# Layer 2 keeps h in the order (batch, node) in a four-layer graph network

## The chip, the cores and the metric

The kernel runs on one core of one Trainium2 chip. The metric is the device time of one execution in microseconds, the median of several runs; smaller is better. Beside the timed runs one execution was recorded by the hardware profiler. All data is fp32.

## The reference

The input x has 128 batches of 64 nodes with 256 features; adj is a 64 by 64 matrix. Four layers follow each other, each as `x = layernorm(x + layer(x))`. Layer 0 is a graph convolution with two linear maps and batch norms. Layer 1 is a spectral step, an attention over the nodes and an MLP. Layer 2, which the change touches, is cut here to what matters:

```python
h = relu(einsum('ts,bsh->bth', adj, x @ Wg0 + bg0))
h = relu(einsum('ts,bsh->bth', adj, h @ Wg1 + bg1))
for p in range(1, MAX_SKIP + 1):                    # 1, 2, 3, 4
    nw = Tv // p                                    # windows of p nodes
    wins = h[:, :nw * p, :].reshape(Bv * nw, p, Hd)
    last = _lstm_last(Wih[p - 1], Whh[p - 1], bih[p - 1], bhh[p - 1], wins)
    idx = jnp.arange(nw) * p + (p - 1)
    h = h.at[:, idx, :].set(last.reshape(Bv, nw, Hd))
```

For each p the 64 nodes of a batch are cut into windows of p nodes. An LSTM runs over the p nodes of every window, and its last state replaces h at the window's last node. Layer 3 is a graph attention that reads `layernorm(x + h)`.

## The kernel before

The 128 batches are cut into 16 blocks of 8 batches (512 rows), and for layer 2 into 4 groups of 32 batches. The state h of a group lies in one SBUF tile `Hg[g]` with the features on the partitions (two halves c of 128) and 64 x 32 positions on the free axis. The view `hT` gives these positions the order (c, node, batch): for one node the 32 batches are neighbours, and the next node is 32 elements (128 bytes) further on.

A planner written in Python (`flow`) sets the order of all instructions. Each piece of work is a generator that yields steps with an engine, an assumed cost, and the number of PSUM tiles and temporary buffers that it takes. The planner picks the next step by these costs and by the free buffers; the engines then run their instructions in the order in which they were written. Several streams compete: graph convolution blocks, LSTM units, weight loads, and the last blocks (layer 3). The final three LSTM units have a stream of their own that is marked urgent.

The parts that matter here:

- `gcn_block(i)` makes h of one block and runs the LSTM for p = 1 on it (one step, no window). Its `out_of` writes the result to `hT_block(i)`, line L1357, on DVE.
- `unit(p, g, w0, nw, b0, nb)` runs the LSTM for p = 2, 3 or 4 on nw windows and nb batches of a group. `units_of` gives 8 units for p = 2 (16 windows each), 8 for p = 3 (12 or 9 windows), and 5 for p = 4 (three of 16 windows and 32 batches, two of 16 windows and 16 batches). `x_of(s, q)` is the view of h at node s of every window, for part q of the unit; units of 32 batches have two parts. `out_of` writes the last state at node p - 1 of every window, line L1389, on DVE.
- `lstm` does the work of a unit. In its first step (s = 0) it multiplies h by the input weights: L1055, with `x_of(0, q)` as the moving operand, as in `T.matmul(out, stationary, moving)`. In the steps after that, a unit with two parts u and v uses products of sums and differences: L1127, of which the product named `A11` has `x_u`, a view of h, as its moving operand; the others move temporaries, save that L1147 (POOL, `T1 = x_v - x_u`) and L1173 (DVE, `T3 = h_v - x_v`) read h to make them.
- `plain_steps` does these steps for the two units of one part (p = 4, group 3): L1264 moves `x`, a view of h, and L1266 moves the LSTM's own state.
- `last_block(i, t0, nt)` is layer 3 for a block, or for half of one in group 3. It first brings h into the order (batch, node) with two copies on ACT (L1467) into a temporary buffer, then transposes it on PE by `to_tm` (L359; the chunk of h is the stationary operand, the identity is moved) and adds it to x (L1478). Later lines: L314 layer normalization on ACT, L308 a power on POOL, L1507 products, L1544 exponentials, L1574 the sum of attention and x.

In the profile's names h is the tile of a group, wL, x and wB hold the weights of p = 1 and 3, 2, and 4 at those products, and t, x, h, rows, wA, wL and others are lent out as temporary buffers too.

Of the kernel before, what the change touches and what calls it, by code (L numbers as in the profile page):

```python
# [11 lines left out]
ALU = mybir.AluOpType  # L12
# [3 lines left out]
P = 128  # L16
B, N, D = 128, 64, 256
# [16 lines left out]
def kernel(ctx: ExitStack, tc: tile.TileContext, a: dict, out: bass.AP):  # L34
    nc = tc.nc
    V, S, G, T = nc.vector, nc.scalar, nc.gpsimd, nc.tensor

    def bc_mid(ap, n):

        return ap.unsqueeze(1).to_broadcast([ap.shape[0], n, ap.shape[1]])  # L40
# [5 lines left out]
    def tm(s):  # L46

        return s.rearrange("p (t d) -> p t d", t=NT)

    def fm(s):  # L50

        return s.rearrange("p (c k) -> p c k", c=2)
# [59 lines left out]
    def mark(*key):  # L112
        done[key] = Clock.end
# [7 lines left out]
    def step(e, us, ps=0, sl=0, waits=True, at=None, tbl=None):  # L121

        return (e, us, ps, sl, waits, at, tbl)
# [83 lines left out]
    def ctile(shape, name, pool=cp):  # L212
        return pool.tile(shape, F32, tag=name, name=name)
# [6 lines left out]
    Hg = [ctile([P, 4 * NT * D], f"h{g}", big) for g in range(NG)]  # L220
    Hs = [Hg[i // 4][:, (i % 4) * NT * D : (i % 4 + 1) * NT * D] for i in range(NBLK)]
    H = [fm(s) for s in Hs]
    hT = [t.rearrange("p (c n b) -> p c n b", c=2, n=N) for t in Hg]
    XD = [dram.tile([P, NT, D], F32, tag=f"xd{i}", name=f"xd{i}") for i in range(NBLK)]

    PS = Stock([ctile([P, NT * D], f"ps{j}", psp) for j in range(4)])
    mem = Stock([ctile([P, NT * D], f"t{j}", big) for j in range(TEMPS)])
# [96 lines left out]
    def joined(ps, n=2 * NT):  # L324

        return ps.rearrange("p (s g e) -> p g s e", s=2, e=N)[:, :n]

    def runs(ap):

        if len(ap.shape) == 2:  # L330
            return ap.rearrange("p (g s e) -> p g s e", s=2, e=N)
        return ap.rearrange("p t (c s e) -> p (t c) s e", s=2, e=N)

    def aggregate(ps, y, mT):


        for c in range(2):
            for t in range(NT):
                for f, to in enumerate(halves):
                    for s, h in enumerate(halves):  # L340
                        T.matmul(  # L341
                            part(ps, s, c * NT + t)[to],
                            y[h, t, c * P + f * N : c * P + (f + 1) * N],
                            mT[h, h],
                            start=True,
                            stop=True,
                        )
# [7 lines left out]
    def to_tm(ps, yT):  # L355

        for t in range(ps.shape[1]):
            for c in range(2):
                T.transpose(ps[:, t, c * P : (c + 1) * P], yT[:, c, t * P : (t + 1) * P], ident)  # L359

    def mm_fm(ps, w, yT, nk, off=0):

        for c in range(2):
            for k in range(nk):
                T.matmul(  # L365
                    ps[:, c, :],
                    w[:, k, (off + c) * P : (off + c + 1) * P],
                    yT[:, k, :],
                    start=(k == 0),
                    stop=(k == nk - 1),  # L370
                )

    def mm_tm(ps, yT, w, nk):

        for t in range(NT):
            for k in range(nk):
                T.matmul(  # L377
                    ps[:, t, :],
                    yT[:, k, t * P : (t + 1) * P],
                    w[:, k, :],  # L380
                    start=(k == 0),
                    stop=(k == nk - 1),
                )

    def by_chunk(ap):
        return ap.rearrange("(k p) m -> p k m", p=P)
# [19 lines left out]
    with c0:  # L406
# [299 lines left out]
        for k, w in zip(("Wc", "Wq", "Wk", "Wv", "Wo", "W1", "W2"), (Wc, Wq, Wk, Wv, Wo, W1, W2)):  # L706
            src = by_chunk(a[f"L1_gnn_{k}"])
# [312 lines left out]

    def hT_block(i):

        return hT[i // 4][:, :, :, (i % 4) * 8 : (i % 4) * 8 + 8]

    def lstm(p, n, parts, x_of, out_of):

# [279 lines left out]
    def gcn_block(i):  # L1306
        yield step("T", 1.15, ps=1, sl=1)
        ps = PS.take()
        s_a = mem.take()
        aggregate(PS[ps], X[i], bdAT)  # L1310
        yield step("Q", 4.0, waits=False)
        nc.sync.dma_start(XD[i], X[i])
        mem.add([Xs[i]], Clock.end, part=("x", i // 2) if i < 8 else None)
        mark("x", i)
        yield step("S", 1.05, ps=-1)
        S.copy(runs(mem[s_a]), joined(PS[ps]))
        PS.give(ps)
        yield step("T", 3.45, ps=1, sl=1)
        ps = PS.take()
        s_h1 = mem.take()  # L1320
        mm_tm(tm(PS[ps]), fm(mem[s_a]), Wg0, 2)
        mem.give(s_a)
        yield step("V", 1.25, ps=-1)
        h1 = tm(mem[s_h1])
        V.tensor_tensor(h1, tm(PS[ps]), bc_mid(rb0, NT), ALU.add)
        PS.give(ps)
        yield step("S", 1.05)
        S.activation(mem[s_h1], mem[s_h1], AF.Relu)
        yield step("T", 1.15, ps=1, sl=1)
        ps = PS.take()  # L1330
        s_a = mem.take()
        aggregate(PS[ps], h1, bdAT)
        mem.give(s_h1)
        yield step("S", 1.05, ps=-1)
        S.copy(runs(mem[s_a]), joined(PS[ps]))
        PS.give(ps)
        yield step("T", 3.45, ps=1, sl=1)
        ps = PS.take()
        s_h2 = mem.take()
        mm_fm(fm(PS[ps]), Wg1, fm(mem[s_a]), 2)  # L1340
        mem.give(s_a)
        yield step("V", 1.4, ps=-1)
        h2 = fm(mem[s_h2])
        for c in range(2):
            V.tensor_tensor(
                h2[:, c, :].rearrange("p (b n) -> p b n", b=8),
                fm(PS[ps])[:, c, :].rearrange("p (b n) -> p b n", b=8),
                bc_mid(rb1[:, c, :], 8),
                ALU.add,
            )  # L1350
        PS.give(ps)
        t = yield step("S", 1.05)
        S.activation(mem[s_h2], mem[s_h2], AF.Relu)  # L1353


        def out_of(q, c, o, th):
            V.tensor_tensor(  # L1357
                hT_block(i)[:, c, :, :].rearrange("p n b -> p b n"), o, th, ALU.mult
            )

        yield step("T", 0.0)
        h2 = h2.rearrange("p c (b n) -> p c b n", b=8)
        yield from lstm(1, TB, [(slice(0, TB), 8)], lambda s, q: h2, out_of)
        yield step("V", 0.0)
        mem.give(s_h2)
        mark("p", 1, i)

    def unit(p, g, w0, nw, b0, nb):
        src = hT[g][:, :, w0 * p : (w0 + nw) * p, b0 : b0 + nb].rearrange("p c (w q) b -> p c w q b", q=p)

        hn = nw * nb // 2
        even = nw % 2 == 0
        parts = [(slice(q * hn, (q + 1) * hn), nw // 2 if even else nw) for q in range(2)]
        if nb < BG:
            parts = [(slice(0, 2 * hn), nw)]

        def half(ap, q):

            if len(parts) == 1:
                return ap  # L1380
            if even:
                return ap[..., q * nw // 2 : (q + 1) * nw // 2, :]
            return ap[..., q * nb // 2 : (q + 1) * nb // 2]

        def x_of(s, q):
            return half(src[:, :, :, s, :], q)

        def out_of(q, c, o, th):
            V.tensor_tensor(half(src[:, c, :, p - 1, :], q), o, th, ALU.mult)  # L1389

        yield from lstm(p, nw * nb, parts, x_of, out_of)
        mark("p", p, g, w0, nw, b0, nb)
# [63 lines left out]
    def last_block(i, t0=0, nt=NT):  # L1456
# [3 lines left out]
        x = tm(mem[s_x])[:, :nt, :]  # L1460
        nc.sync.dma_start(x, XD[i][:, t0 : t0 + nt, :])
        r = nt / NT
        yield step("S", 2.2 * r, sl=1)
        s_h = mem.take()
        hb = fm(mem[s_h])[:, :, : nt * P]
        for c in range(2):
            S.copy(  # L1467
                hb[:, c, :].rearrange("p (b n) -> p b n", n=N),
                hT_block(i)[:, c, :, 2 * t0 : 2 * (t0 + nt)].rearrange("p n b -> p b n"),
            )  # L1470
        yield step("T", 0.9 * r, ps=1)
        ps = PS.take()
        px = tm(PS[ps])[:, :nt, :]
        to_tm(px, hb)
        mem.give(s_h)
        mark("read", i)
        yield step("V", 0.1 + 1.2 * r, ps=-1)
        V.tensor_tensor(x, px, x, ALU.add)  # L1478
# [6 lines left out]
        px = fm(PS[ps])[:, :, : nt * P]  # L1485
# [99 lines left out]
    seq, n = [], 0  # L1585
# [73 lines left out]
    for p, g in [(2, g) for g in range(NG)] + [(3, 0), (3, 1), (4, 0), (3, 2), (4, 1), (3, 3), (4, 2), (4, 3)]:  # L1659
        if p == 2:  # L1660
            need = [("p", 1, i) for i in range(4 * g, 4 * g + 4)] + [("begun", NBLK - 1)]
        else:
            need = units_of(p - 1, g)
        for u in units_of(p, g):
            units.append((lambda p=p, need=need: ready(("w", p), *need), lambda u=u: unit(*u[1:]), 7))
# [5 lines left out]
    def last_of(i, *part):  # L1671
        return (lambda: ready(("wx",), *units_at_end(i)), lambda: last_block(i, *part), 3)
# [66 lines left out]
```

## Time and profile before

| what | value |
|---|---|
| median of 3 runs (lowest to highest) | 2407.23 us (2405.26 to 2409.41) |
| profiled execution, its time | 2409.44 us |
| its span | 2407.7 us |
| mean granted TensorE clock | 0.982 |
| instructions | 40,603 |
| L1467, the copies ahead of layer 3 | 24 of 512 elements, 16 of 256; first at 1859.6, last at 2375.8 us |
| L1357, p = 1 writing h | 32 of 512 elements, from 464.3 to 1356.7 us |
| first product of a p = 2 unit | 1214.9 us |
| first product of a p = 4 unit | 1718.1 us |

PE is TensorE's multiplication and PEld its loading of stationary operands; DVE is VectorE, ACT ScalarE, POOL GpSimd, and SP the engine that starts most transfers. A group of instructions is shown as line, engine, operation, out<-in, shape and count, then busy time and the mean duration of one in ns, then how long the engine was idle just before and who ended that. Every `T.matmul` of the program appears as two MATMUL records. The records of matmuls that follow each other overlap, so the time of one is read from the distance between starts.

### The profile page before, as it was taken

The numbers are of one execution on the slowest core, as the hardware profiler recorded it, in microseconds if no ns is written. First come the engines' busy times: TensorE is split into PE (matmuls) and PEld (weight loads), VectorE is DVE, ScalarE is ACT, GpSimd is POOL, SyncE is SP. The second block draws the span as 40 slices with busy tenths as digits, with TensorE's granted clock in tenths as the row PEclk, the third lists the DMA queues.
The fourth block names the chain that finished last, engine by engine and source line by source line (L and its number), as shares of the span: only waits on it lengthen the run. The fifth ranks groups of instructions, "written<-read, shape, count | busy, mean of one in ns | idle before, by whom it ended". The sixth has DMA issues, their size and how long they took to land.

```text
span 2407.7 us, 40603 instructions
## 1 busy us (share of the span) xinstructions
PE 2287.2 (95%) x16916; PEld 1759.9 (73%) x16916; DVE 1287.7 (53%) x2904; ACT 1187.4 (49%) x2189; POOL 591.7 (25%) x441
## 2 busy tenths in 40 slices
PE   8999788999989999999999999999999999998997
PEld 4548665666665666666667788899999888887785
DVE  4557678566483474744643433454444444455546
ACT  2257643544434544335453443444444653468766
POOL 0012134232242232331321222222221222122122
PEclk9999899999999999999999999999999999999998
DMA  6100301000000000001000000000001000001111
GB/s 162 49 1 1 111 23 49 28 10 10 1 12 17 10 10 10 1 10 36 36 19 27 18 1 1 17 2 1 1 1 36 1 10 9 19 27 66 40 36 45
DMA packets 42633, 57.91 MB, mean 24 GB/s; under 512 B 6224, under 2 KB 35536, under 8 KB 42448
## 3 DMA queue, kind: packets, MB, share of 16 engines
q1 hardware_dynamic: 41344, 54.22, 7.0%
q8 instruction: 133, 2.18, 0.4%
q10 hardware_dynamic: 1104, 1.08, 0.1%
q14 instruction: 52, 0.43, 0.1%
HBM read 38.52 MB, written 16.78 MB: 23 GB/s over the span
## 4 chain that ended last, share of the span: by engine, by line
PE 60%; DVE 16%; ACT 7%; POOL 3%; issue 2%; POOLq 0%; ACTq 0%; DVEq 0%
PE ps L1127 26%; PE ps L1055 11%; PE ps L365 7%; PE ps L377 4%; PE ps L938 4%; DVE ln_st L272 3%; ACT x L314 2%; PE ps L808 2%; POOL ln_rs L308 1%; PE ps L1507 1%; DVE x L300 1%; PE ps L341 1%; DVE ln_mv L273 1%; PE ps L353 1%; DVE ln_nm L311 1%
## 5 line engine op out<-in xcount | busy, mean ns | idle before, releaser
L1127 PE MATMUL ps<-x,x 128*128 128x256 f32 x928 | 225.0, 380 | 0.7 <-DVE t L1195 0.7
L1127 PEld LDWEIGHTS ps<-x,x 128*128 128x128 f32 x928 | 173.5, 190 | 24.9 <-issue 1.6
L314 ACT ACTIVATE x<-x,ln_nm,ln_rs 128x256 f32<-128x256 f32 x212 | 112.3, 592 | 133.3 <-DVE ln_nm L311 131.9
L1127 PE MATMUL ps<-t,x 128*128 128x256 f32 x672 | 163.7, 380 | 0.0
L1127 PEld LDWEIGHTS ps<-t,x 128*128 128x128 f32 x672 | 126.4, 190 | 17.1 <-DVE x L1195 0.8
L308 POOL TENSOR_TENSOR ln_rs<-ln_rs,neghalf 128x4 f32<-128x4 f32 (+1 forms) x72 | 71.2, 990 | 212.0 <-DVE ln_rs L274 186.4
L365 PE MATMUL ps<-t,W1T 128*128 128x512 f32 x256 | 117.8, 607 | 0.0
L1055 PE MATMUL ps<-h,wL 128*128 128x192 f32 (+2 forms) x480 | 103.9, 371 | 4.8 <-ACT h L1353 4.8
L272 DVE BATCH_NORM_STATS2 ln_st<-x 128x6 f32<-128x256 f32 x260 | 99.7, 403 | 0.4
L1055 PEld LDWEIGHTS ps<-h,wL 128*128 128x128 f32 x480 | 75.6, 192 | 29.9 <-issue 22.5
L294 POOL TENSOR_TENSOR ln_rs<-ln_rs,neghalf 128x4 f32<-128x4 f32 x32 | 36.9, 1153 | 217.1 <-DVE ln_rs L274 217.0
L1055 PE MATMUL ps<-h,x 128*128 128x256 f32 x384 | 86.7, 380 | 2.2 <-ACT t L1067 1.8
L1067 ACT ACTIVATE t<-ps,bih 128x512 f32<-128x512 f32 (+3 forms) x98 | 57.2, 634 | 55.8 <-PE ps L1055 55.1
L1203 ACT ACTIVATE x<-x,bih 128x512 f32<-128x512 f32 (+2 forms) x69 | 44.6, 648 | 80.3 <-DVE x L1193 80.0
L1186 DVE COPY x<-ps 128x256 f32<-128x256 f32 (+2 forms) x69 | 26.1, 378 | 108.4 <-PE ps L1127 107.6
L365 PEld LDWEIGHTS ps<-t,W1T 128*128 128x128 f32 x256 | 47.6, 195 | 49.6 <-issue 49.5
L365 PE MATMUL ps<-t,wA 128*128 128x512 f32 x160 | 76.8, 626 | 5.5 <-ACT t L784 5.5
L1055 PEld LDWEIGHTS ps<-h,x 128*128 128x128 f32 x384 | 72.6, 190 | 12.9 <-ACT t L1067 2.2
L1186 DVE COPY t<-ps 128x256 f32<-128x256 f32 (+2 forms) x51 | 18.8, 373 | 103.8 <-PE ps L1127 103.5
L1067 ACT ACTIVATE x<-ps,bih 128x512 f32<-128x512 f32 (+3 forms) x86 | 51.5, 650 | 40.6 <-PE ps L1055 40.4
L273 DVE BATCH_NORM_AGGREGATE ln_mv<-ln_st 128x2 f32<-128x6 f32 x448 | 71.3, 167 | 0.0
L1193 DVE TENSOR_TENSOR x<-ps,x 128x512 f32<-128x512 f32 (+2 forms) x69 | 41.4, 602 | 53.0 <-PE ps L1127 43.6
(714 smaller groups left out, 5713.2 us busy)
## 6 DMA issues: line engine op xcount, KB each, us to landing
t<-in_x_dram SPq DMA_DIRECT2D x26, 512.0 KB, 4.3
xd<-x SPq DMA_DIRECT2D x16, 512.0 KB, 2.6
x<-xd SPq DMA_DIRECT2D x8, 512.0 KB, 3.3
out_dram<-x SPq DMA_DIRECT2D x8, 512.0 KB, 2.9
h<-in_x_dram SPq DMA_DIRECT2D x5, 512.0 KB, 5.2
wL<-in_L_gnn_Wih_dram SPq DMA_DIRECT2D x2, 1024.0 KB, 5.0
x<-in_L_gnn_Whh_dram SPq DMA_DIRECT2D x2, 1024.0 KB, 5.4
x<-xd SPq DMA_DIRECT2D x5, 256.0 KB, 2.9
```

The costliest lines, as they stand in the source:

```text
L272: V.bn_stats(st[:, t, :], y[:, t, :])
L273: V.bn_aggr(mv[:, t, :], st[:, t, :])
L308: G.tensor_tensor(rs, rs, neghalf[:, :n], ALU.pow)
L314: S.activation(y[:, t, :], y[:, t, :], AF.Identity, scale=rs[:, t : t + 1], bias=nm[:, t : t + 1])
L365: T.matmul(ps[:, c, :], w[:, k, (off + c) * P : (off + c + 1) * P], yT[:, k, :], start=(k == 0), stop=(k == nk - 1),)
L377: T.matmul(ps[:, t, :], yT[:, k, t * P : (t + 1) * P], w[:, k, :], start=(k == 0), stop=(k == nk - 1),)
L808: T.matmul(pv[r * N : (r + 1) * N, b, :, :], x1T[:, k, b * N : (b + 1) * N], Wv_par[:, k, r, :, :], start=(k == 0), stop=(k == 1),)
L938: T.matmul(tm(PS[ps])[:, t, :], fm(mem[gs[k // 2]])[:, k % 2, t * P : (t + 1) * P], W2[:, k, :], start=(k == 0), stop=(k == 3),)
L1055: T.matmul(spread(fm(PS[ps])[:, j, :n], q), WL[p][0][:, k, m], x_of(0, q)[:, k], start=(k == 0), stop=(k == 1),)
L1067: S.activation(of(sl)[:, j], fm(PS[ps])[:, j, :n], AF.Tanh if g == 2 else AF.Sigmoid, bias=bias(g, c))
L1127: T.matmul(dst, WS[p][name](k, g), y[:, k], start=first and k == 0, stop=k == 1, skip_group_check=not first)
L1186: V.tensor_copy(y[:, 1, :], v[:, 0, :])
```

## The change

The view `hT` gets the order (c, batch, node). For one batch the 64 nodes are now neighbours, and the next batch is 64 elements on. All readers and writers of h follow:

- p = 1 writes whole blocks in storage order.
- In `unit`, the windows' node s is now a view with a step of p elements inside a batch. The two parts of a unit are always split by batch; before, they were split by windows where the number of windows is even.
- `last_block` loses its copies, the step on ACT and the temporary buffer; the transposes read h from the group's tile.

```diff
-    hT = [t.rearrange("p (c n b) -> p c n b", c=2, n=N) for t in Hg]
+    hT = [t.rearrange("p (c b n) -> p c b n", c=2, n=N) for t in Hg]
...
-        return hT[i // 4][:, :, :, (i % 4) * 8 : (i % 4) * 8 + 8]
+        return hT[i // 4][:, :, (i % 4) * 8 : (i % 4) * 8 + 8]
...
-            V.tensor_tensor(
-                hT_block(i)[:, c, :, :].rearrange("p n b -> p b n"), o, th, ALU.mult
-            )
+            V.tensor_tensor(hT_block(i)[:, c], o, th, ALU.mult)
...
-        src = hT[g][:, :, w0 * p : (w0 + nw) * p, b0 : b0 + nb].rearrange("p c (w q) b -> p c w q b", q=p)
+        src = hT[g][:, :, b0 : b0 + nb, w0 * p : (w0 + nw) * p].rearrange("p c b (w q) -> p c b w q", q=p)
...
-        even = nw % 2 == 0
-        parts = [(slice(q * hn, (q + 1) * hn), nw // 2 if even else nw) for q in range(2)]
+        parts = [(slice(q * hn, (q + 1) * hn), nb // 2) for q in range(2)]
         if nb < BG:
-            parts = [(slice(0, 2 * hn), nw)]
+            parts = [(slice(0, 2 * hn), nb)]
...
-            if even:
-                return ap[..., q * nw // 2 : (q + 1) * nw // 2, :]
-            return ap[..., q * nb // 2 : (q + 1) * nb // 2]
+            return ap[..., q * nb // 2 : (q + 1) * nb // 2, :]
...
-            return half(src[:, :, :, s, :], q)
+            return half(src[..., s], q)
...
-            V.tensor_tensor(half(src[:, c, :, p - 1, :], q), o, th, ALU.mult)
+            V.tensor_tensor(half(src[:, c, :, :, p - 1], q), o, th, ALU.mult)
...
-        yield step("S", 2.2 * r, sl=1)
-        s_h = mem.take()
-        hb = fm(mem[s_h])[:, :, : nt * P]
-        for c in range(2):
-            S.copy(
-                hb[:, c, :].rearrange("p (b n) -> p b n", n=N),
-                hT_block(i)[:, c, :, 2 * t0 : 2 * (t0 + nt)].rearrange("p n b -> p b n"),
-            )
         yield step("T", 0.9 * r, ps=1)
         ps = PS.take()
         px = tm(PS[ps])[:, :nt, :]
-        to_tm(px, hb)
-        mem.give(s_h)
+        to_tm(px, hT_block(i)[:, :, 2 * t0 : 2 * (t0 + nt)].rearrange("p c b n -> p c (b n)"))
```

## The prediction

> **What bounds the kernel now.** I read three views first: engine totals, the table of windows, and the chain of waits.
>
> ```profile
> PE 2287.2 (95%) x16916; PEld 1759.9 (73%) x16916; DVE 1287.7 (53%) x2904; ACT 1187.4 (49%) x2189; POOL 591.7 (25%) x441
> ```
>
> ```profile
> 1200.00:1350.00 150.00, 145.63 (x975) 105.11 (x974) 62.61 (x132) 66.15 (x108) 32.63 (x23) 1.00 0.05 18
> 1350.00:2100.00 750.00, 747.05 (x4085) 677.76 (x4084) 335.60 (x656) 347.23 (x788) 173.11 (x126) 1.00 0.03 9
> 2100.00:2250.00 150.00, 137.64 (x946) 119.13 (x945) 87.70 (x270) 112.89 (x261) 33.41 (x34) 0.99 0.13 42
> 2250.00:2408.00 158.00, 136.29 (x845) 110.29 (x843) 79.64 (x308) 110.77 (x267) 31.74 (x45) 0.96 0.13 42
> ```
>
> Columns after the window are its length, then busy time with count of PE, PEld, DVE, ACT and POOL. From 1350 to 2100 us, where the LSTM units of p = 2, 3 and 4 run, PE lacks 3 us of 750, with the full clock granted (1.00). Only after 2100 does PE idle, 12.4 + 21.7 = 34 us; there ACT is busy 73% of the time. So a nanosecond added to the LSTM's matmuls is paid almost whole, and a microsecond taken from ACT counts only after 2100.
>
> PE means in the groups overlap, so the rate comes from the chain of waits (start, length, what), which in 1350 to 1600 follows the very matmuls whose moving operand is h:
>
> ```profile
> 1362.76 3.45 PE ps L1055 x16
> 1564.33 2.60 PE ps L1055 x16
> 1584.88 1.96 PE ps L1055 x16
> ```
>
> These are p = 2 (256 columns), p = 3 (192) and p = 3 (144): 215.6, 162.5 and 122.5 ns each, so (215.6 - 122.5)/112 = 0.83 ns a column, with next to no fixed part. Now the moving operand is read in runs of 32 or 16 adjacent elements.
>
> Which operations already read or write SBUF with a large step?
>
> ```profile
> L1467 ACT COPY x<-h 128x512 f32<-128x512 f32 x10 | 10.4, 1094 | 0.0
> L1467 ACT COPY t<-h 128x512 f32<-128x512 f32 x8 | 8.6, 1096 | 0.0
> L1467 ACT COPY t<-h 128x256 f32<-128x256 f32 x4 | 2.4, 630 | 2.5 <-DVE ln_rs L274 2.5
> L1467 ACT COPY x<-h 128x256 f32<-128x256 f32 x2 | 1.2, 638 | 0.0
> L1203 ACT ACTIVATE x<-x,bih 128x512 f32<-128x512 f32 x35 | 25.1, 718 | 51.3 <-DVE x L1193 51.2
> L1205 ACT ACTIVATE x<-x,bih 128x256 f32<-128x256 f32 x35 | 17.1, 494 | 0.0
> L1357 DVE TENSOR_TENSOR h<-x,x 128x512 f32<-128x512 f32 x5 | 5.0, 1064 | 6.5 <-ACT x L1067 6.5
> L1173 DVE TENSOR_TENSOR t<-x,h 128x512 f32<-128x512 f32 x4 | 2.7, 684 | 0.0
> ```
>
> The copies of L1467 read h 128 bytes apart: (1095 - 634)/256 = 1.80 ns an element, while the contiguous L1203/L1205 take (718 - 494)/256 = 0.88. L1357 writes h 128 bytes apart: 1064 against 684 ns for 512 elements adjacent, so 0.74 more than DVE's own 1.04 ns (from 512 and 256 elements, 684 and 418 ns), 1.78 together. Two engines of different pace, one reading, one writing, meet the same 1.79 ns an element. That looks like a price of the memory, not of the engine.
>
> **What the Trainium skill says.** "Advanced Engine Details and Errata", section Memory Cachelines, has lines of 16 bytes in SBUF, full speed while accesses stay in a line, and at least two hits on a line needed to absorb the memory's latency. The 1.79 ns above agree. "SBUF — State Buffer", section Door 1, adds that one can stride for free up to 4 fp32, which for a step of 4 contradicts two hits a line; no run shows which is right, nor whether PE pays at all. "TensorE: Matmul & The Clock Gate", Part 2, gives the streaming operand an SBUF read port of its own and N cycles of streaming; the trace agrees with time proportional to N. "GPSIMD Engine Reference", section 7, charges half again as much for steps over 8 bytes; no row here shows it.
>
> **The change part by part.**
>
> *Removed: the copies before layer 3.* 24 x 1.09 + 16 x 0.64 = 36 us of ACT, one planner step and one buffer a block. Before 2100 (12 copies) other PE work hides them: gain nothing. After 2100 (12 long and 16 short) the chain itself holds them for 1.1 us near 2193 and 4.2 us in 2300 to 2306. If the copies go, the next late thing there is ACT's own queue (layer normalization L314 and table loads) and PE. I take 5 us, bounds 0 and 12.
>
> *p = 1 writes (L1357) become adjacent.* 32 x 0.38 = 12 us of DVE less, in 460 to 1357, where PE is 96% busy and only one instruction waited 1.5 us for this line: 1 us, bounds 0 and 4.
>
> *h read or written with a step of p elements by DVE and POOL.* A step of 8, 12 and 16 bytes touches 0.5, 0.75 and 1 new line an element; at 1.79 ns a line that is 0.90, 1.34 and 1.79 ns. Against DVE's 1.04: L1173 (8 instructions of 384, 8 of 288 for p = 3, 9 of 512 for p = 4) pays 1.6 + 3.5 us, L1389 (16 of 192, 16 of 144, 16 of 256) 1.6 + 3.1. POOL's L1147 (1264 ns for 512) by the skill's half more: 9 x 0.63 for p = 4 and 16 x about 0.45 for p = 3, 13 us. DVE is under half busy there and POOL under a quarter, and no PE wait was put down to L1147: zero, bounds 0 and 8. If that cover were gone the whole 23 us would be paid.
>
> *PE's moving operand with a step of p elements.* The stationary operand of the last transposes stays adjacent (two batches of 64 nodes), at no cost. The instructions that read h, each product being two in the trace:
>
> ```profile
> L1055 PE MATMUL ps<-h,wB 128*128 128x256 f32 x192 | 43.0, 380 | 0.3 <-ACT t L1494 0.3
> L1127 PE MATMUL ps<-h,wB 128*128 128x256 f32 x144 | 37.9, 385 | 0.9 <-ACT t L1207 0.9
> L1264 PE MATMUL ps<-h,wB 128*128 128x256 f32 x192 | 50.4, 385 | 1.9 <-ACT t L1269 1.1 <-DVE x L1478 0.6
> L1055 PE MATMUL ps<-h,wL 128*128 128x192 f32 x192 | 33.3, 327 | 0.0
> L1127 PE MATMUL ps<-h,wL 128*128 128x192 f32 x128 | 26.6, 330 | 0.0
> L1055 PE MATMUL ps<-h,x 128*128 128x256 f32 x384 | 86.7, 380 | 2.2 <-ACT t L1067 1.8 <-ACT t L1316 0.4
> ```
>
> - p = 4: 192 + 144 + 192 = 528 of 256 columns, 135,168 columns.
> - p = 3: 320 of 192 (shown) and 320 of 144, 107,520 columns.
> - p = 2: 384 (shown) and 128 in L1127 (8 units x 4 gates x 2 halves x 2), 131,072 columns.
>
> No row shows PE with a small step, so both ends: 0 if its fetch runs ahead, and 1.79 - 0.83 = 0.96 ns on every column, 359 us. I take the price by lines: 0.96 x 135,168 = 130 us; (1.34 - 0.83) x 107,520 = 55; (0.90 - 0.83) x 131,072 = 8, total 193. Of this, 240 instructions (59 us) belong to group 3's p = 4 units in the tail; PE has 34 us idle there, but the urgent LSTM chain is itself what the tail waits for, so I let 7 us be absorbed.
>
> *Waits.* The transposes (L359) now wait for DVE's L1389 directly instead of for ACT's copy of it; what stands behind them on PE waits no longer than before, and the group's buffers come free at the same mark, after the transposes. No DMA is added or moved.
>
> *Order.* With a step gone, the planner lays the instructions out anew from the first last_block on (1860 us), and p = 3's short units split by batch in both halves. Zero, bounds -5 and +8.
>
> **Sum:** 193 - 7 - 5 - 1 = +180 us. The profiled execution took 2409.4 us (span 2407.7); the median of the runs is 2407.2. So 2587 us.
>
> **Rivals.**
>
> *A, forecast: PE pays by lines for all steps.* 2587 us, its own range 2550 to 2612. For it: the same 1.79 ns on two engines, and PE's 0.83 ns a column, as fast as ACT's element, which leaves no slack. Against: PE's port is not measured.
>
> *B: only the step of 16 bytes pays*, the 12-byte step being absorbed by the one line in three that is hit twice: 130 - 13 = +117, 2524 us.
>
> *C, other side: PE's fetch hides the steps.* Neighbouring lines might lie in different banks, which a step of 128 bytes can't tell. Then only the copies count: -6 us, 2401, range 2392 to 2412. It decides as soon as PE pays less than 6/373,760 us, 0.016 ns a column: even the 8 us of p = 2 would outweigh the gain. The skill's "4 fp32" speaks for it.
>
> *D: every step pays a whole line*: 359 - 13 = +346, 2753 us.
>
> That the copies don't go is excluded: they are deleted from the text, and the transposes read h itself.
>
> **How the numbers follow.** A 0.38, B 0.20, C 0.35, D 0.07. Under C the new order could undo 6 us, so C splits into 0.26 faster, 0.05 within 0.2%, 0.04 slower; 0.2% (5 us) is about what a measurement of this kernel can tell from no change. Slower: 0.38 + 0.20 + 0.07 + 0.04 = 0.69. The range has to reach from C to A: 2394 to 2612, leaving out D and the edges.
>
> **What would show it.** In the chain of waits sixteen products of L1055 at p = 4 should take 16 x 458 = 7.3 us instead of 3.45, at p = 3 of 192 columns 4.1 instead of 2.6, at p = 2 3.7. L1467 is gone; p = 1's DVE write is near 684 ns; L1389 with 256 elements at p = 4 is near 610. PE should still be near 95% busy. If the sixteen at p = 4 stay at 3.45 us, the forecast is wrong and C holds; if p = 3 stays at 2.6, B.

## The result, and the profile after

The changed kernel takes 2574.9 us (median of 4 runs, 2573.26 to 2575.9) against 2407.24 us before; the ratio is 1.0696, 95% interval 1.0677 to 1.0714. It is slower by 168 us. The profiled execution has a span of 2572.7 us against 2407.7.

The engine totals of the kernel after come first, then its table of windows (length, then busy time with count of PE, PEld, DVE, ACT and POOL, the granted clock and the DMA share):

```profile
PE 2464.9 (96%) x16916; PEld 1803.6 (70%) x16916; DVE 1290.9 (50%) x2904; ACT 1154.2 (45%) x2145; POOL 612.0 (24%) x441
```

```profile
1350.00:2100.00 750.00, 748.80 (x3578) 621.82 (x3578) 309.41 (x578) 297.45 (x683) 171.20 (x114) 1.00 0.02 7
2100.00:2250.00 150.00, 146.66 (x703) 119.21 (x702) 64.60 (x136) 61.75 (x143) 33.53 (x21) 0.99 0.04 15
2250.00:2573.00 323.00, 298.93 (x1584) 209.48 (x1582) 146.07 (x520) 176.70 (x443) 52.35 (x68) 0.97 0.12 38
```

PE has the same 16,916 instructions and is busy 177.7 us longer (2464.9 - 2287.2). In the 750 us from 1350 on it gets through 3578 matmuls where the kernel before got through 4085, at the same full clock. PEld, DVE, ACT and POOL are all busy for less time there, since PE sets the pace. ACT as a whole lost 33 us, because the copies are gone.

The chain of waits of the kernel after (start, length, what) has the same products that the prediction showed:

```profile
1358.21 3.47 PE ps L1055 x16
...
1566.89 4.16 PE ps L1055 x16
...
1585.93 3.41 PE ps L1055 x16
...
1758.06 7.22 PE ps L1055 x16
```

From the top these are p = 2 (256 columns), p = 3 (192), p = 3 (144) and p = 4 (256): 216.9, 260, 213 and 451 ns each, where the chain before gave 215.6, 162.5, 122.5 and, again, 215.6. The p = 4 products in the chain before:

```profile
1725.68 3.45 PE ps L1055 x16
```

The same groups in the list by shapes confirm the counts; busy time is the first number after the bar:

```profile
L1264 PE MATMUL ps<-h,wB 128*128 128x256 f32 x192 | 94.9, 628 | 0.0
...
L1055 PE MATMUL ps<-h,x 128*128 128x256 f32 x384 | 88.8, 383 | 2.4 <-ACT t L1067 2.0 <-ACT t L1316 0.4
L1055 PE MATMUL ps<-h,wB 128*128 128x256 f32 x192 | 88.0, 629 | 0.0
...
L1127 PE MATMUL ps<-h,wB 128*128 128x256 f32 x144 | 71.8, 634 | 0.6 <-DVE x L1464 0.4 <-ACT t L1207 0.2
```

The p = 4 groups went from 50.4, 43.0 and 37.9 us to 94.9, 88.0 and 71.8; p = 2 hardly moved, from 86.7 to 88.8. By the distances between starts, PE's price is 528 x 235 ns for p = 4, 320 x 98 and 320 x 91 ns for p = 3, and 512 x 1.3 ns for p = 2: 124 + 31 + 29 + 1 = 185 us.

Two groups of the kernel after are off PE. In the first, p = 1 now writes h adjacently and DVE takes 687 ns instead of 1064. In the second, POOL's T1 reads h with a step:

```profile
L1357 DVE TENSOR_TENSOR h<-x,x 128x512 f32<-128x512 f32 x5 | 3.3, 687 | 6.5 <-ACT x L1067 6.5
...
L1147 POOL TENSOR_TENSOR t<-h 128x512 f32<-128x512 f32 x9 | 16.9, 1881 | 18.0 <-PE ps L1127 12.4 <-DVE t L1102 4.6 <-ACT t L1094 0.7
```

### The profile page after: what moved, and what is told of

Same layout as the page of the kernel before. It is cut to its first block, busy times and chain, and to the rows that moved or that the text cites. A ratio compares the mean times of both kernels' runs of the same rounds, so it can differ in the third digit from the quotient of the medians.

```text
span 2572.7 us, 40552 instructions
## 1 busy us (share of the span) xinstructions
PE 2464.9 (96%) x16916; PEld 1803.6 (70%) x16916; DVE 1290.9 (50%) x2904; ACT 1154.2 (45%) x2145; POOL 612.0 (24%) x441
## 4 chain that ended last, share of the span: by engine, by line
PE 69%; DVE 12%; ACT 3%; POOL 2%; issue 2%; POOLq 0%; ACTq 0%; DVEq 0%
PE ps L1127 27%; PE ps L1055 15%; PE ps L365 7%; PE ps L938 4%; PE ps L1264 3%; PE ps L377 3%; DVE ln_st L272 2%; PE ps L1493 2%; PE ps L1266 2%; PE ps L808 1%; PE ps L353 1%; DVE x L300 1%; PE ps L341 1%; ACT x L314 1%; POOL ln_rs L308 1%
## 5 line engine op out<-in xcount | busy, mean ns | idle before, releaser
L1127 PE MATMUL ps<-t,x 128*128 128x256 f32 x864 | 210.4, 380 | 0.0
L1127 PEld LDWEIGHTS ps<-t,x 128*128 128x128 f32 x864 | 162.4, 190 | 29.4 <-issue 9.7
L314 ACT ACTIVATE x<-x,ln_nm,ln_rs 128x256 f32<-128x256 f32 x176 | 93.8, 593 | 129.1 <-DVE ln_nm L311 128.9
L1055 PE MATMUL ps<-h,wL 128*128 128x192 f32 (+2 forms) x480 | 138.6, 450 | 4.8 <-ACT h L1353 4.8
L1127 PE MATMUL ps<-x,x 128*128 128x256 f32 x576 | 140.1, 380 | 0.6 <-DVE t L1195 0.6
L1055 PEld LDWEIGHTS ps<-h,wL 128*128 128x128 f32 x480 | 94.3, 198 | 42.0 <-issue 21.7
L1127 PEld LDWEIGHTS ps<-x,x 128*128 128x128 f32 x576 | 108.5, 190 | 20.2 <-issue 4.6
L1264 PE MATMUL ps<-h,wB 128*128 128x256 f32 x192 | 94.9, 628 | 0.0
L1055 PE MATMUL ps<-h,x 128*128 128x256 f32 x384 | 88.8, 383 | 2.4 <-ACT t L1067 2.0
L1055 PE MATMUL ps<-h,wB 128*128 128x256 f32 x192 | 88.0, 629 | 0.0
L272 DVE BATCH_NORM_STATS2 ln_st<-x 128x6 f32<-128x256 f32 x224 | 85.6, 402 | 0.4
L1127 PE MATMUL ps<-h,x 128*128 128x256 f32 x320 | 80.4, 380 | 0.2 <-ACT x L1335 0.2
```

What stands on the lines that cost most here:

```text
L272: V.bn_stats(st[:, t, :], y[:, t, :])
L314: S.activation(y[:, t, :], y[:, t, :], AF.Identity, scale=rs[:, t : t + 1], bias=nm[:, t : t + 1])
L1055: T.matmul(spread(fm(PS[ps])[:, j, :n], q), WL[p][0][:, k, m], x_of(0, q)[:, k], start=(k == 0), stop=(k == 1),)
L1127: T.matmul(dst, WS[p][name](k, g), y[:, k], start=first and k == 0, stop=k == 1, skip_group_check=not first)
L1264: T.matmul(shaped(dst), WL[p][0][:, k, m], x[:, k], start=(k == 0), stop=False)
```

## Experiments

The theory: PE pays for every 16-byte line of SBUF that its moving operand touches, and that is the whole loss. The rivals: the planner's new order, the steps of DVE and POOL, or a price at the 16-byte step alone. Ratios are to the kernel before, run on the same chip (medians 2407.99 and 2408.15 us).

**PE adjacent, all else as changed.**

```diff
+        pe_of = lambda s, q: half(hT[g][:, :, b0 : b0 + nb, w0 * p + s * nw : w0 * p + (s + 1) * nw], q)
...
-                            x_of(0, q)[:, k],
+                            pe_of(0, q)[:, k],
...
-                product(g, "A11", x_u, shaped(v[:, 0, :]), first=True)
+                product(g, "A11", pe_of(s, 0), shaped(v[:, 0, :]), first=True)
...
-            yield from plain_steps(p, n, us, of, bias, x_of, lambda ap: spread(ap, 0), last_h, s_cell, s_h, h_at)
+            yield from plain_steps(p, n, us, of, bias, pe_of, lambda ap: spread(ap, 0), last_h, s_cell, s_h, h_at)
```

> The changed kernel, in which only PE's moving operand is read from 9 to 16 adjacent elements of the same unit's h instead of with a step of p (so PE multiplies the wrong nodes); DVE and POOL still step by p, the copies are still gone, the order of the instructions stays that of the changed kernel. Theory (PE pays for the step, by lines): the 185 us that the two traces give for PE's products go away, 2390 us (2380 to 2400), below the kernel before. Rival (the new order of the planner, or the steps of DVE and POOL, made the time): stays near 2575.

Measured: 2410.8 us, ratio 1.0010 (1.0003 to 1.0017). PE's busy time is that of the kernel before (2287.2):

```profile
PE 2286.7 (95%) x16916; PEld 1762.6 (73%) x16916; DVE 1298.2 (54%) x2904; ACT 1149.0 (48%) x2145; POOL 611.5 (25%) x441
```

So the loss goes away with PE's step alone, and order, DVE and POOL are not the cause of more than a few us of it. But 2390 was a miss: taking 185 us of instruction time off PE gave back 164 us, not 185, and left nothing of a gain.

**PE with a step, all else as before.**

Shortened:

```diff
+        flat = ...   # the unit's own adjacent part of the group's tile
+        pe_of = lambda s, q: flat[part q].rearrange("p c (k r) -> p c k r", r=p)[..., s]
```

The three places that take `pe_of` are those of the experiment above.

> The kernel before, with its layout, copies and order, in which only PE's moving operand is read with a step of p elements from the unit's own part of h (so PE multiplies the wrong nodes). Theory: PE alone brings 528 x 0.235 + 320 x (0.0975 + 0.0905) = 184 us, less what idle time of PE absorbs: 2585 us (2570 to 2595). Rival (order, DVE, POOL): stays near 2407.

Measured: 2574.2 us, ratio 1.0692 (1.0676 to 1.0708), the time of the changed kernel. PE's busy time is 178.1 us more than before:

```profile
PE 2465.3 (96%) x16916; PEld 1802.7 (70%) x16916; DVE 1283.0 (50%) x2904; ACT 1192.9 (46%) x2189; POOL 593.6 (23%) x441
```

The old order and the old copies with PE's step alone make the whole loss.

**No copies, no step.** The copies, their step in the planner and their buffer go; the layout stays.

```diff
-        yield step("S", 2.2 * r, sl=1)
-        s_h = mem.take()
-        ...
-        to_tm(px, hb)
-        mem.give(s_h)
+        o = (i % 4) * TB + t0 * P
+        to_tm(px, Hg[i // 4].rearrange("p (c k) -> p c k", c=2)[:, :, o : o + nt * P])
```

> The kernel before without the copies ahead of layer 3 and their step in the planner; the transposes read adjacent elements of the group's tile, in the order (node, batch), so layer 3 gets rows in a wrong order. No step of p anywhere; the planner gives the order of the changed kernel. Theory: the gain of the change by itself; the 165 us measured against 185 on PE leave about 20, so 2388 us (2380 to 2400). By the prediction's 5 us for the copies: 2402. Rival (copies hidden): 2407.

Measured: 2402.65 us, ratio 0.9984 (0.9975 to 0.9992), 5.3 us faster. By the medians that is the prediction's 5 us for the copies, with the new order in it. 2388 was a miss: the 20 us that I had read into the difference between PE's instructions and the span are not there.

**p = 4 adjacent.** `pe_of` of the first experiment where p is 4, `x_of` else.

> The changed kernel, with PE's moving operand adjacent for p = 4 alone (so the units of p = 4 multiply the wrong nodes); p = 2 and p = 3 keep their steps. Theory (price by lines, additive): 528 x 0.235 = 124 us less, 2451 us (2440 to 2462). Rival that only a step of 16 bytes pays: the whole excess goes, 2390. Rival (order): 2575.

Measured: 2459.4 us, ratio 1.0217 (1.0201 to 1.0232). So p = 4 brings 115.5 us of its 124, and what is left over the first experiment, 48.6 us, is p = 3's and p = 2's (61 by instruction time). A price at 16 bytes alone is ruled out: a step of 12 bytes pays too.

**Bursts.** A kernel of bursts, each of 16 matmuls (32 records) on a line of its own, such as

```python
for o, wt, x in pe(256, mv(256, 4, 1), st(1)): T.matmul(o, wt, x, start=True, stop=True)
```

with 256 columns, step 4 in runs of 1, and a stationary operand with step 1.

> A small kernel of bursts alone (it computes none of the network; its output is filler): 16 fp32 matmuls of 64 to 512 columns whose moving operand has a step of 1 to 32 elements or runs of 2, stationary operands with a step of 1 to 32, ACT copies, DVE products and POOL products with steps of 1 to 32. Theory (a price for every 16-byte line of SBUF, 1.77 ns): PE takes 0.83 ns a column at step 1, 0.85 to 0.89 at step 2 and in runs of 2, 1.33 at step 3, 1.77 at step 4, and no more at 5, 6, 8, 16 and 32; ACT the same 1.77 from step 4 on. Rival (neighbouring lines lie in different banks): PE at step 4 is faster than at 8 or 16. Rival (each byte of step costs): keeps growing beyond step 4. For stationary operands: no cost up to step 2 and 128 x 1.77 = 227 ns from step 4 on by lines, against nothing if their port is different.

The chain of waits of this kernel, of which the lines are: L56 to L60 steps 1, 2, 3, 4 and 5, L62 step 8, L64 step 32, L65 runs of 2 with step 4; L71 128 columns with step 3; L77 step 4 with 512 columns; L79, L81 and L82 are 64 columns with a stationary operand of step 1, 3 and 4.

```profile
62.30 6.91 PE ps L56 x32
69.20 7.25 PE ps L57 x32
76.45 10.88 PE ps L58 x32
87.33 14.44 PE ps L59 x32
101.77 14.61 PE ps L60 x32
...
130.78 14.72 PE ps L62 x32
...
159.30 13.87 PE ps L64 x32
173.17 7.25 PE ps L65 x32
...
209.10 5.54 PE ps L71 x32
...
279.15 28.80 PE ps L77 x32
...
337.32 3.52 PE ps L79 x32
...
344.61 6.05 PE ps L81 x32
350.66 7.45 PE ps L82 x32
```

Steps 1 to 4 take 215.9, 226.6, 340 and 451 ns a record, and then it stays within 5% of that: 457, 460 and 433 at steps 5, 8 and 32. From 256 to 512 columns at step 4 the chain grew from 14.44 to 28.80 us, 1.75 ns a column; step 3 gives (10.88 - 6.91)/32 = 124 ns more, where 0.75 x 1.75 - 0.83 = 0.48 ns on 256 columns makes 124. So the price is 1.75 ns a line. Neighbouring lines in different banks would have been fast at step 4 and slow at 8 or 32; no such thing is seen.

The rows of the moving operand all ran at a granted clock of 1.00; near 348 us, within L81, it fell to 0.50. The windows of L79 and L82:

```profile
337.32:340.84 3.52, 3.52 (x34) 3.52 (x33) 0.00 (x0) 0.00 (x0) 0.00 (x0) 1.00 0.02 5
```

```profile
350.66:358.10 7.44, 7.44 (x33) 7.44 (x34) 0.00 (x0) 0.00 (x0) 0.00 (x0) 0.50 0.00 0
```

So L82's 233 ns can't be set against L79's 110: at half the clock the latter would be 220, an estimate that takes it to go with the clock. Ahead of 348 us the records of L81 start 173 ns apart. That is the 173 ns of L71, where 128 moving columns have step 3: a stationary operand of 128 columns pays for a step of 3 too. What a step of 4 costs there at the full clock was not measured.

The other engines in the same kernel: ACT reading 512 elements at step 1 (L91) and 4 (L94) and 256 at step 4 (L88), DVE writing them at 1 (L97) and 4 (L100), POOL reading both operands at 1, 3 and 4 (L109, L111, L112), in the list by shapes.

```profile
L94 ACT COPY za<-y 128x512 f32<-128x512 f32 x4 | 4.6, 1138 | 0.1
...
L88 ACT COPY za<-y 128x256 f32<-128x256 f32 x4 | 2.6, 656 | 0.1
...
L91 ACT COPY za<-y 128x512 f32<-128x512 f32 x4 | 2.5, 618 | 0.1
...
L100 DVE TENSOR_TENSOR zd<-y 128x512 f32<-128x512 f32 x4 | 4.4, 1111 | 0.0
...
L97 DVE TENSOR_TENSOR zd<-y 128x512 f32<-128x512 f32 x4 | 2.7, 682 | 0.0
...
L112 POOL TENSOR_TENSOR zg<-zd,y 128x512 f32<-128x512 f32 x4 | 8.4, 2107 | 0.3
...
L111 POOL TENSOR_TENSOR zg<-zd,y 128x512 f32<-128x512 f32 x4 | 7.1, 1774 | 0.3
...
L109 POOL TENSOR_TENSOR zg<-zd,y 128x512 f32<-128x512 f32 x4 | 5.0, 1262 | 47.5 <-DVE zd L102 47.2
```

All pay at step 4. ACT takes (1138 - 656)/256 = 1.88 ns an element there. DVE takes (1111 - 682)/512 = 0.84 ns an element more than at step 1, which makes 1.88 with the 1.04 of the prediction. Both are near PE's 1.75 but not equal to it. For POOL, which read two operands with a step, no price a line follows from this.

**POOL adjacent too.** From the first experiment:

```diff
-            G.tensor_tensor(shaped(T1), x_v, x_u, ALU.subtract)
+            G.tensor_tensor(shaped(T1), pe_of(s, 1), pe_of(s, 0), ALU.subtract)
```

> The changed kernel with PE's moving operand and also POOL's T1 reading adjacent elements (wrong nodes are multiplied and subtracted); DVE still steps by p. It splits the 8 us between the changed kernel with PE adjacent (2410.8) and the kernel before without copies (2402.7). If POOL's longer T1 (1.6 instead of 1.26 us) is what delays: 2403 to 2405. If DVE's writes and reads are: 2410.

Measured: 2403.7 us, ratio 0.9983 (0.9975 to 0.9992), against 1.0003 to 1.0017 with POOL's step: by the medians 7 us are POOL's. The windows from 1560 to 2100, first with POOL's step, then without:

```profile
1560.00:2100.00 540.00, 530.62 (x3106) 490.56 (x3105) 269.31 (x512) 247.56 (x599) 146.28 (x97) 1.00 0.03 11
```

```profile
1560.00:2100.00 540.00, 533.59 (x3127) 493.50 (x3126) 264.85 (x515) 248.41 (x601) 136.26 (x100) 1.00 0.03 11
```

POOL is busy 10 us less and PE, the first busy time, works 3 us more of the 540. The profiles show less than the medians: in both, matmul record 12,000 (counted from 0 in order of start) starts at 1558.4 us, and from there the one without POOL's step ends 2.7 us sooner (span 2405.4 against 2408.1). So POOL's step costs 3 to 7 us. DVE's steps leave about 1 us to the kernel without copies (2402.65), within the scatter of the runs.

The traces show how large that scatter is. Matmul record 3000 comes before p = 1 first writes h (459 us at the earliest), so no layout or step of these experiments can have touched it, and yet it starts between 417.1 and 422.1 us in the nine profiled executions of the network. A difference of a few us between two executions may come from there.

**Pairs and quads.** If lines are what costs, h can lie so that both readers are content. Here the batches are laid in groups of 2 or 4 neighbours inside a node; with 4, these are the four row tiles t of a block, so that a transpose still reads one free axis, with a step of 4 elements. The edit for quads, shortened:

```diff
-    hT = [t.rearrange("p (c b n) -> p c b n", c=2, n=N) for t in Hg]
+    hT = [t.rearrange("p (c b n l) -> p c b n l", c=2, n=N, l=4) for t in Hg]
...
-        return hT[i // 4][:, :, (i % 4) * 8 : (i % 4) * 8 + 8]
+        return Hg[i // 4].rearrange("p (c b t m l) -> p c b t m l", c=2, b=4, t=1, l=4)[:, :, i % 4]
...
-        to_tm(px, hT_block(i)[:, :, 2 * t0 : 2 * (t0 + nt)].rearrange("p c b n -> p c (b n)"))
+        hb = hT_block(i)
+        for t in range(nt):
+            for c in range(2):
+                T.transpose(px[:, t, c * P : (c + 1) * P], hb[:, c, 0, :, t0 + t], ident)
```

For p = 2 and 3 the differences on POOL and DVE are made one half c at a time. With pairs:

> The changed kernel with another layout of h: (c, two-batch group, node, 2 batches), so that a step of p nodes still finds 2 adjacent elements, and the last transposes read their stationary operand with a step of 2 elements; no copies. POOL's and DVE's differences are made in two instructions for p = 2 and 3. Theory (price by lines, 2 hits absorb it nearly): PE's products take 217 to 228 ns for 256 columns, so 2400 to 2425 us; the gain without copies, 5 us, is just about eaten if 2 hits cost 0.06 ns a column on 373,760 columns. Rival (any step other than 1 costs PE a lot): 2570.

Measured: 2416.2 us, ratio 1.0037 (1.0023 to 1.0052). Its chain of waits has sixteen p = 2 products at 3.62 us, 226 ns each, the 226.6 of L65 in the bursts: two hits a line are not quite free, and 4 ns (p = 3 with 144 columns) to 14 ns (p = 4) more on the 1680 records outweigh the copies.

> As the layout with pairs, but with 4 adjacent batches: (c, group, node, 4 batches). PE's moving operand, POOL and DVE then read whole lines, and only the last transposes have a step, of 4 elements, on their stationary operand. Theory: products at 215.6 ns; 256 loads of a stationary operand take up to 227 instead of 107 ns, in part under other matmuls: 0 to 31 us on the 2402.7 of the kernel without copies, so 2400 to 2430. If a stationary operand doesn't pay for a step: 2400 to 2405, a little faster than the kernel before.

Measured: 2403.9 us, ratio 0.9980 (0.9972 to 0.9988): 4.2 us faster than before and 171 us faster than the changed kernel. The chain of waits of this kernel, p = 2, p = 3 (192), p = 3 (144), p = 4, and eight transposes with a stationary step of 4:

```profile
1424.15 3.45 PE ps L1055 x16
...
1562.51 2.60 PE ps L1055 x16
...
1660.82 1.96 PE ps L1055 x16
...
1723.85 3.45 PE ps L1055 x16
...
1898.57 0.96 PE ps L1467 x8
```

The products are back at their old rates, and the eight transposes take 0.96 us where the kernel without copies has 0.87: 16 blocks' worth costs 1.4 us. This version beats both kernels; what it gains on the kernel before is about what the kernel without copies gains.

## Why the prediction was right, point by point

- **What bounds.** Right: PE, and a price on its moving operand is paid for some nine tenths. PE alone, in the old order, makes 166 of the 168 us.
- **The price by lines from ACT and DVE.** Right in kind and nearly in size: 1.75 ns measured on PE, against 1.79 inferred. The sum by instruction was 185 us for 193. The term that was mis-sized most is p = 2: 8 us forecast, 1 measured, since 216.9 ns is nearly the old 215.6. p = 3 cost what was forecast at 192 columns (97.5 ns more a record, forecast 98) and more at 144 (213 ns, where 7 lines for each run of 9 elements, 112 lines in all, give 196): 60 us for 55. p = 4: 124 for 130. That the price holds on PE was not certain beforehand: A had 0.38, C 0.35.
- **What the tail absorbs.** Too small: I let 7 us be absorbed, and 20 of the 185 don't reach the end. From 2100 us on PE's idle time fell from 34.1 to 27.4, near those 7. Over the whole span it fell by 12.7 (120.5 to 107.8), but 4.5 of these lie ahead of 1200 us (79.4 to 74.9), where PE reads h with no step: that part is scatter. The other 7 of the 20 lie between the 185 of the starts and the 177.7 of busy time, and 4 of them come from the sum itself: paired record by record with the first experiment, which has the same order but for 8 records, the products that read h gain 181 us (p = 4 122, p = 3 58), not 185. In the same pairing all other distances between starts lose 17 us, 5 of them ahead of record 3000. So by this working some 12 us came back as shorter waits.
- **The copies.** Right in size, as far as it can be told: 5 us forecast, 5.3 by the medians with all else unchanged but the order. From matmul record 3000 on, the two profiles differ by 2.4 us only (2407.7 - 422.1 against 2400.3 - 417.1), so the close match is luck. That p = 1's write became adjacent was not tested alone.
- **POOL and DVE at zero.** Wrong by 3 to 7 us, inside the bound of 8: POOL's longer T1 delays the kernel, though in the profile of the changed kernel only 0.2 us of waiting, once and by PEld, are put down to L1147. The step that failed was to take the absence of such a wait for a cover. The way the delay takes was not shown; T1 stands at the head of POOL's queue, and L1086 and L1220 behind it are on the units' path. In the changed kernel it about cancels the copies: PE's step alone gives 2574.2 us, the full change 2574.9. DVE's writes of 256 elements at p = 4 (L1384 now) took 605 to 647 ns, near the 610 forecast, and cost nothing that a run could tell.
- **Order.** Not tested apart; with the copies it is inside the 5.3 us.
- **Rivals.** B falls with the 48.6 us of the 12-byte step and the 340 ns of the burst; C and the sentence of the Trainium skill that speaks for it ("SBUF — State Buffer", section Door 1, strides up to 4 fp32 free) fall with the 451 ns at step 4. What "Advanced Engine Details and Errata", section Memory Cachelines, says, two hits a line, agrees nearly: 226.6 ns at step 2 against 215.9. D falls with p = 2. The half more that "GPSIMD Engine Reference", section 7, charges for steps over 8 bytes is about met at step 3, 1262 to 1774, but at step 4 it is two thirds more, 2107.

The terms measured apart add up to +166 (PE) - 5 (copies and order) + 7 (POOL) + 1 (DVE) = +169, against 168. The last three are differences of successive kernels and must add up to the 2.8 us of the first experiment; what the sum tests is that PE's step costs the same in the old order (166) as in the new (164). The forecast of +180 is 12 too high: PE's term is 20 too high (186 after what is absorbed, for 166), and the 8 us (by the medians) of POOL and DVE, which had been put at zero, happen to make up for part of it.

## What to carry to other kernels

A view with a step in its last axis is not free for TensorE just because the number of columns is the same: count the 16-byte lines that the moving operand touches, and price them, as a first estimate, from any engine of the same trace that already reads with a step (1.79 ns here, 1.75 on PE itself). Where two readers want different orders, look for a layout that keeps a full line (here four fp32) together for the heavy reader and leaves the step to the light one. And a copy that is taken off a free engine is worth only what the end of the kernel waits for it, 5 of 36 us here.

## What the runs showed that I had not expected

- A step of 2 in a straight row costs 226.6 ns for 256 columns, but in the changed kernel, where each run of 16 elements is followed by a gap of 128 bytes, only 216.9. And runs of 9 elements with step 3 cost 213 ns for 144 columns, where a straight row in the experiment with PE's step alone took 193 (3.09 us for 16). Lines alone don't explain this; it was not followed further.
- A stationary operand with a step costs time too: 173 ns a record at step 3 in matmuls of 64 columns, against 110, at the full clock. In the transposes of the quads kernel, also at a granted clock of 1.00, a step of 4 lengthens the records of the loads from 141 to 213 ns, but only 11 ns a transpose come through.
- The granted clock fell to half within the last bursts, and the chain of waits doesn't show it: there 233 ns looks like the price of a step. The clock of a stretch has to be read beside its times.
- POOL pays at step 2 already: 1492 ns (L110) against 1262.
